# VectorE takes the sums over W2 behind its part of the second block's first einsum

## The chip, the cores and the metric

The kernel runs on one core of one Trainium2 chip. The metric is the time on the device, in microseconds (us), of one execution; the median of several runs is given. TensorE does the matmuls, VectorE (DVE) and ScalarE (ACT) the elementwise work, GpSimd (POOL) casts weights and issues the stores, SyncE (SP) issues the loads.

## The reference, cut to what matters

```
w   = weights[conditions]                     # (128, 64, 64), one matrix for each of 128 samples
xc  = einsum('bct,bcd->bdt', x, w)            # first einsum; x is (128, 64, 512)
W1q = ternarize(W1); W2q = ternarize(W2)      # W1 (2048, 512), W2 (512, 2048)
h   = gelu(einsum('bsd,hd->bsh', xc, W1q) + b1)
y   = einsum('bsd,hd->bsh', h, W2q) + b2
out = x + fp4(y)      # y rounded to multiples of max|y| / 7 + 1e-8

ternarize(W):
    delta = 0.05 * max|W|
    mask  = |W| > delta
    alpha = sum(|W| where mask) / max(count(mask), 1)
    return alpha * sign(W) * mask
```

The kernel keeps the signs (-1, 0 or 1) as weights and applies alpha to the result. So alpha of W2, the sum of the kept magnitudes over their count, is wanted only when the first results y are made.

## The kernel before

*Tiling.* The 128 samples are cut into 16 blocks of 8. A block is four pairs of samples, j = 0 to 3; two samples fill the 128 partitions, and the block has 512 tokens. The hidden layer's 2048 columns are 16 chunks of 128, hc = 0 to 15. W1 and W2 are handled in four groups g of four chunks each.

*Order.* Each engine takes its instructions in the order in which the program writes them. There is no planner: `InOrder` keeps every instruction in program order on its engine, and semaphores join the engines. Moving a line in the program moves that instruction in its engine's queue. As every operation is recorded by that helper, all rows of the profile name line 55; they are told apart by their tiles.

*The first einsum.* `condition(n, j, ...)` is made for each pair: `mix` lets TensorE multiply x by a block-diagonal matrix into a PSUM tile `pc`; ScalarE copies `pc` to the high part `x0`, and VectorE subtracts the high part from `pc` to get the low part `x1` (`split`). In the rows of the profile these are `pc<-diag,xt`, `x<-pc` and `x<-pc,x`. The pool `ps_c` has two PSUM buffers, used by `pc` and by a few small tiles such as `total2`.

*The two layers.* `layer1(n, hc)` multiplies both parts by a chunk of W1 into `ph`; ScalarE applies gelu and VectorE makes the low part of h (`h<-ring,h`); `layer2(n, hc)` multiplies h by a chunk of W2 into four PSUM tiles `py`. POOL widens each chunk of the weights beforehand (`widen1`, `widen2`; rows `wf<-...`), into two or four buffers that TensorE sets free.

*Around the change.* Block 0 is unlike the others: its layer 1 runs while W2 is still being made ternary, so its layer 2 comes afterwards in one loop over hc = 0 to 13 (lines 643 to 666). Beside this loop's matmuls

- VectorE makes the last two groups of W2 ternary (`signed2(2)` at hc = 0, `signed2(3)` at hc = 3; rows `junk<-nat` and `terns<-nat`),
- for each group g, at hc = 4, 6, 8 and 9, ScalarE counts the kept weights (`count2`, rows `masks<-terns`) and stores them in eight bits (`kept`, rows `w2t<-terns`), and VectorE sums them (`sum2`, rows `nat<-nat,terns`, with a read of the accumulator, `sums<-`),
- at hc = 5, 7, 9 and 11 the first einsum of block 1 is done, one pair j each.

Then `eight` goes on with block 1 and the last two chunks of block 0's layer 2. At its second step (`s == NH + 1`) `alpha_2` lets TensorE add the sums and counts over the partitions in a small matmul, `total`; VectorE makes alpha of W2 from it and then the results of block 0.

Of the kernel before, what the change touches and what calls it, by code (L numbers as in the profile page):

```python
# [58 lines left out]
def tile_cond_ternary_ffn(  # L59
# [141 lines left out]
    def parts(n):  # L201
        return [big.tile([P, NT, BLK], F32R, tag="big", name=f"x{k}_{n}") for k in range(2)]

    def split(src, hi, lo, engine=dve):

        act.copy(hi, src)
        engine.tensor_tensor(lo, src, hi, ALU.subtract)

    def pair_of(xt, j):
        return xt[j // 2][:, j % 2, :]  # L210

    def mix(xp, j, pc):

        for c in range(NT):
            pe.matmul(
                out=pc[:, c, :],
                lhsT=xp[:, c * P : (c + 1) * P],
                rhs=diag[:, j, :],
                start=True,
                stop=True,  # L220
            )

    def condition(n, j, xp, two):
        pc = ps_c.tile([P, NT, P], F32, tag="pc", name=f"pc_{n}_{j}")
        mix(xp, j, pc)
        split(pc, *(t[:, :, j * P : (j + 1) * P] for t in two))
# [30 lines left out]
    def flat(w):  # L257
        return w.rearrange("p a b -> p (a b)")
# [130 lines left out]
    def widen2(n, hc):  # L389
        if n == 0 and hc < NH - LAG:  # L390
            w = w2f[hc % 4]
        elif n == NB - 1 and hc == NH - 1:

            w = flat(w1f[0])
        else:
            w = w2f[hc % 2]
        if n == 0 and hc < NH - LAG:
            g, i = divmod(hc, GH)
            pool.tensor_copy(w, group1(terns2, g)[:, i * T : (i + 1) * T])
        else:  # L400
            pool.tensor_copy(w, w2t[:, hc])
        wide2[n, hc] = w
# [28 lines left out]
    def low(n, hc):  # L431

        open_low.pop((n, hc), lambda: None)()

    def layer2(n, hc, js=range(PAIRS)):
        two = hidden[n, hc]
        w = wide2[n, hc]
        if n not in ypsum:
            ypsum[n] = [
                ps_y.tile([P, T], F32, tag=f"py{j}", name=f"py{j}_{n}") for j in range(PAIRS)  # L440
            ]
        for j in js:
            for k in range(2):
                pe.matmul(
                    out=ypsum[n][j],
                    lhsT=two[k][:, j * P : (j + 1) * P],
                    rhs=w,
                    start=(hc == 0 and k == 0),
                    stop=(hc == NH - 1 and k == 1),
                )  # L450
# [56 lines left out]
    def group2(g):  # L507
        return group1(terns2, g)
# [6 lines left out]
    def signed2(g):  # L515

        delta2, minus2 = delta
        below = junk[:, g % 2, :]
        if g % 2 == 0:
            terns2.append(big.tile([P, 2, WCH], BF16, tag="big", name=f"terns2_{g}"))  # L520
        dve.tensor_scalar(below, flat(nat2[g]), minus2, None, ALU.is_lt)
        dve.scalar_tensor_tensor(
            group2(g), flat(nat2[g]), delta2, below, ALU.is_gt, ALU.subtract
        )

    def count2(g):
        act.activation(
            group1(masks, 2 + g % 2), group2(g), AF.Square, accum_out=sums2[:, 1, g : g + 1]
        )

    def sum2(g):
        dve.tensor_tensor_reduce(
            out=flat(nat2[g]),
            in0=flat(nat2[g]),
            in1=group2(g),
            scale=1.0,
            scalar=0.0,
            op0=ALU.mult,
            op1=ALU.add,
            accum_out=sums2[:, 0, g : g + 1],  # L540
        )
# [97 lines left out]
    def kept(t, g, tiles):  # L639

        act.copy(flat(t[:, g * GH : (g + 1) * GH]), group1(tiles, g), saturate=False)

    for hc in range(NH - LAG):
        if hc + 2 < NH - LAG:
            widen2(0, hc + 2)
        layer2(0, hc)
        if hc == 0:
            signed2(2)
        if hc == 1:
            for i in range(10, NH):  # L650
                low(0, i)
        if hc < NG:
            kept(w1t, hc, terns)
        if hc == 3:
            signed2(3)
        if hc == 4:
            two_next = parts(1)
            w2t = big.tile([P, NH, T], F8, tag="big", name="w2t")
        if hc in (4, 6, 8, 9):
            g = {4: 0, 6: 1, 8: 2, 9: 3}[hc]  # L660
            count2(g)
            kept(w2t, g, terns2)
            sum2(g)
        if hc in (5, 7, 9, 11):
            j = (hc - 5) // 2
            condition(1, j, pair_of(x_next, j), two_next)
    cond[1] = two_next
    x_next, two_next, fetched = [], [], []
    hf = ring[:2]
# [296 lines left out]
    while s < len(steps):  # L966
        n, hc = steps[s]
# [133 lines left out]
```

## Time and profile before

| what | value |
|---|---|
| median of 3 runs | 1058.8 us (1058.51 to 1059.65) |
| profiled execution's own time | 1058.49 us |
| its span, first to last instruction | 1056.6 us |
| TensorE busy | 985.9 us, 93% of the span |
| VectorE, ScalarE, POOL busy | 609.9, 612.0 and 625.6 us |
| granted TensorE clock, mean | 0.970; 1.00 in each stretch before 985 us |
| the changed loop's sums on VectorE | four, 2.28 us in the median, from 72.0 to 82.4 us |
| last stage, from about 985 us | loads and stores, TensorE nearly idle |

A row of the profile's order of time gives the start in us, the duration in us, the engine, the line, the operation, what it writes and reads, its shape, and how many alike are merged into it. In square brackets stands how long the engine was idle before it, and what ended that idleness. Rows of one engine overlap a little, since the next instruction begins before the last one's end is recorded. A list of waits gives, for each pair of engine and releaser, the total in us, the number of times and the longest.

### The profile page before, as it was taken

What the parts mean: (1) busy time and instruction counts of PE and PEld (TensorE: products, weight loads), DVE (VectorE), ACT (ScalarE), POOL (GpSimd) and SP (SyncE); (2) the same over time, 40 slices, a digit from 0 to 9 for tenths busy, and PEclk for the clock granted to TensorE, in tenths of its full rate; (3) what the DMA queues carried; (4) which work ended last, traced back from release to release, by engine and by line L of the source; (5) the groups of instructions that cost most, each with busy time, mean ns of one, the idle gap of its engine ahead of it and who ended that gap; (6) DMA issues with size and microseconds to landing.
All of it is one profiled execution on the core that took longest, in us unless ns stands there. A gap on an engine that the chain in (4) does not pass through costs nothing.

```text
span 1056.6 us, 16741 instructions
## 1 busy us (share of the span) xinstructions
PE 985.9 (93%) x5768; PEld 864.5 (82%) x5769; DVE 609.9 (58%) x1081; ACT 612.0 (58%) x1045; POOL 625.6 (59%) x1017
## 2 busy tenths in 40 slices
PE   8999999999999999999999999999999999999500
PEld 5877889999999999999999999999898888888400
DVE  7896645565656565666656565666655223231692
ACT  7993546666666565656666565656555333443591
POOL 6865656676766667676666767576664435333242
PEclk9999999999999999999999999999999999999755
DMA  9100100100000010101000010101001010051799
GB/s 361 59 21 4 32 13 15 31 6 31 15 22 23 14 32 7 39 6 32 15 22 23 14 33 4 41 7 30 16 22 43 3 41 6 1 181 39 264 413 376
DMA packets 26628, 62.21 MB, mean 59 GB/s; under 512 B 3504, under 2 KB 3504, under 8 KB 25776
## 3 DMA queue, kind: packets, MB, share of 16 engines
q1 hardware_dynamic: 19872, 42.25, 12.1%
q0 software_dynamic: 6672, 18.88, 4.7%
q8 instruction: 47, 0.77, 0.3%
q14 instruction: 37, 0.30, 0.1%
HBM read 44.34 MB, written 16.78 MB: 58 GB/s over the span
## 4 chain that ended last, share of the span: by engine, by line
PE 89%; DVE 5%; DMA 3%; ACT 1%; issue 1%; SPq 0%; POOLq 0%; DVEq 0%; ACTq 0%
PE py L55 42%; PE xy L55 16%; PE ph L55 13%; PE z L55 12%; PE pc L55 5%; DMA out<-y 3%; DVE y L55 1%; DVE h L55 1%; ACT diag L55 1%; DMA nat<-in_L_ffn_W 1%; DVE top L55 1%; DVE junk L55 1%; DVE terns L55 0%; PE number L55 0%; DVE ymax L55 0%
## 5 line engine op out<-in xcount | busy, mean ns | idle before, releaser
L55 PE MATMUL py<-wf,h 128*128 128x512 f32 x2048 | 530.7, 395 | 0.0
L55 PEld LDWEIGHTS py<-wf,h 128*128 128x128 f32 x2048 | 365.4, 189 | 63.5 <-DVE y L55 1.9
L55 DVE TENSOR_TENSOR h<-ring,h 128x512 fp32r<-128x512 f32 x236 | 182.7, 777 | 142.7 <-ACT h L55 142.7
L55 POOL CAST wf<-w2t 128x512 fp32r<-128x512 fp8e4 x242 | 169.6, 701 | 152.0 <-PE py L55 148.1
L55 ACT ACTIVATE ring<-ring,b1t,alpha_w 128x512 f32<-128x512 f32 x176 | 144.3, 820 | 97.9 <-DVE ring L55 97.9
L55 POOL CAST wf<-w1s 128x256 fp32r<-128x256 fp8e4 (+1 forms) x264 | 133.8, 511 | 110.2 <-PE xy L55 80.7
L55 POOL CAST wf<-w1t 128x256 fp32r<-128x256 fp8e4 (+1 forms) x240 | 158.5, 665 | 59.4 <-PE ph L55 47.8
L55 PE MATMUL ph<-x,wf 128*128 128x512 f32 (+1 forms) x656 | 157.6, 385 | 0.3 <-DVE x L55 0.3
L55 ACT CAST h<-ring 128x512 fp32r<-128x512 f32 x240 | 148.9, 621 | 7.8
L55 PEld LDWEIGHTS ph<-x,wf 128*128 128x128 f32 x656 | 120.6, 188 | 25.5 <-POOL wf L55 0.7
L55 DVE TENSOR_TENSOR ring<-xy,ring 128x256 f32<-128x256 f32 (+1 forms) x176 | 97.3, 553 | 64.3 <-PE xy L55 64.3
L55 PEld LDWEIGHTS xy<-xt,wf 128*128 128x128 f32 x704 | 107.6, 189 | 14.1
L55 PE MATMUL xy<-xb,wf 128*128 128x256 f32 x704 | 112.4, 281 | 0.0
L55 PE MATMUL xy<-xt,wf 128*128 128x256 f32 x704 | 111.8, 282 | 0.0
L55 ACT ACTIVATE ring<-ph,b1t,alpha_w 128x512 f32<-128x512 f32 x64 | 49.8, 778 | 106.3 <-PE ph L55 106.2
L55 PEld LDWEIGHTS xy<-xb,wf 128*128 128x128 f32 x704 | 102.2, 190 | 7.9
L55 ACT COPY ring<-xy 128x256 f32<-128x256 f32 x176 | 65.1, 370 | 68.1 <-PE xy L55 68.0
L55 PE MATMUL z<-xt,wf 128*128 128x256 f32 x704 | 98.3, 282 | 0.0
L55 ACT COPY ring<-z 128x512 f32<-128x512 f32 x88 | 51.7, 588 | 73.6 <-DVE h L55 71.4
L55 PEld LDWEIGHTS z<-xt,wf 128*128 128x128 f32 x704 | 90.2, 190 | 0.0
L55 DVE TENSOR_TENSOR xt<-x_quarters,xt 128x512 fp32r<-128x512 f32 x44 | 33.8, 767 | 90.9 <-ACT xt L55 90.9
L55 POOL DMA_INDIRECT wg<-in_L_cond_weights,rows x64 | 73.2, 1143 | 11.8 <-issue 7.7
(108 smaller groups left out, 886.8 us busy)
## 6 DMA issues: line engine op xcount, KB each, us to landing
xt<-in_x SPq DMA_DIRECT2D x36, 512.0 KB, 7.0
out<-y POOLq DMA_DIRECT2D x29, 512.0 KB, 12.3
x_quarters<-in_x SPq DMA_DIRECT2D x48, 256.0 KB, 2.6
nat<-in_L_ffn_W SPq DMA_DIRECT2D x6, 1024.0 KB, 10.3
nat<-in_L_ffn_W SPq DMA_DIRECT2D x3, 512.0 KB, 8.8
wg<-in_L_cond_weights,rows POOLq DMA_INDIRECT x64, 2.7
w1t<-in_x SPq DMA_DIRECT2D x4, 256.0 KB, 2.7
w2t<-in_x SPq DMA_DIRECT2D x4, 256.0 KB, 2.6
```

Of the source, the lines that this page charges most:

```text
L55: return lambda *args, **kw: self._tc.keep_in_program_order(make(*args, **kw))
```

## The change

The call of `sum2(g)` at hc = 4, 6, 8 and 9 is taken out. The sums are now called behind `condition(1, j)`: the sum of group 0 behind j = 1 (hc = 7), of group 1 behind j = 2 (hc = 9), of groups 2 and 3 behind j = 3 (hc = 11). `count2` and `kept` stay where they were. As `count2`, `kept` and `condition` keep their order, only VectorE's queue changes.

```diff
@@ -660,10 +660,11 @@
             g = {4: 0, 6: 1, 8: 2, 9: 3}[hc]
             count2(g)
             kept(w2t, g, terns2)
-            sum2(g)
         if hc in (5, 7, 9, 11):
             j = (hc - 5) // 2
             condition(1, j, pair_of(x_next, j), two_next)
+            for g in {7: [0], 9: [1], 11: [2, 3]}.get(hc, []):
+                sum2(g)
     cond[1] = two_next
     x_next, two_next, fetched = [], [], []
     hf = ring[:2]
```

VectorE's order in this part, from the end of `signed2(3)` on:

| before | after |
|---|---|
| sum2(0), low part j = 0 | low part j = 0, low part j = 1 |
| sum2(1), low part j = 1 | sum2(0), low part j = 2 |
| sum2(2), sum2(3) | sum2(1), low part j = 3 |
| low part j = 2, low part j = 3 | sum2(2), sum2(3) |

## The prediction

> **What bounds the kernel now.** I read three views in this order: busy time and the chain of waits, for what sets the end; what TensorE waited for, for its holes; and the order of time around the largest hole, engine by engine.
>
> ```profile
> PE 985.9 (93%) x5768; PEld 864.5 (82%) x5769; DVE 609.9 (58%) x1081; ACT 612.0 (58%) x1045; POOL 625.6 (59%) x1017
> PE 89%; DVE 5%; DMA 3%; ACT 1%; issue 1%; SPq 0%; POOLq 0%; DVEq 0%; ACTq 0%
> ...
> PE pc L55 <- DVE x L55: 1.2, 1, 1.2
> ```
>
> TensorE carries 89% of the chain and is busy nearly without a break up to the tail that starts near 985 us, so only its own work and holes count. The list of its waits has one hole inside the dense part that this edit can touch: a first-einsum matmul (`pc`) of block 1 that waited 1.2 us, once, for a VectorE subtract into `x`. Its place on TensorE:
>
> ```profile
> 65.25 3.89 PE L55 MATMUL py<-wf,h 128*128 128x512 f32 x16
> 68.98 1.05 PE L55 MATMUL pc<-diag,xt 128*128 128x128 f32 x8
> 69.79 3.89 PE L55 MATMUL py<-wf,h 128*128 128x512 f32 x16
> 74.90 1.16 PE L55 MATMUL pc<-diag,xt 128*128 128x128 f32 x8 [1.23 <-DVE x L55]
> 75.81 3.89 PE L55 MATMUL py<-wf,h 128*128 128x512 f32 x16
> 79.54 1.05 PE L55 MATMUL pc<-diag,xt 128*128 128x128 f32 x8
> 80.35 3.89 PE L55 MATMUL py<-wf,h 128*128 128x512 f32 x16
> ```
>
> These are `layer2(0, hc)` two at a time, with `mix` for j = 1, 2, 3 between. And VectorE's queue:
>
> ```profile
> 69.39 2.64 DVE L55 SCALAR_TENSOR_TENSOR terns<-nat,delta_w,junk 128x2048 bf16<-128x2048 f32 x1
> 71.95 2.28 DVE L55 CUSTOM_DVE_ANT_0 nat<-nat,terns 128x2048 f32<-128x2048 f32 x1
> ...
> 74.17 0.68 DVE L55 TENSOR_TENSOR x<-pc,x 128x512 fp32r<-128x512 f32 x1
> 74.77 2.63 DVE L55 CUSTOM_DVE_ANT_0 nat<-nat,terns 128x2048 f32<-128x2048 f32 x1
> ...
> 82.36 1.27 DVE L55 TENSOR_TENSOR x<-pc,x 128x512 fp32r<-128x512 f32 x2
> ```
>
> `CUSTOM_DVE_ANT_0` is `sum2`; `x<-pc,x` is the low part of `condition`, call them lo0 to lo3. `ps_c` has two buffers, so the third `pc` can't start until lo0 has read the first. lo0 ends at 74.85 and the `pc` starts at 74.90. lo0 was late because `sum2(0)` stood in front of it. ScalarE's copy that lo0 also needs was done at 66.58 (66.00 + 0.58), so nothing else held it.
>
> **The change part by part.** It adds and removes nothing: four `sum2`, their four accumulator reads and four lo subtracts only trade places on VectorE. The queues of TensorE, ScalarE, POOL and SP keep their order, so no DMA is moved. The new VectorE order is lo0, lo1, sum2(0), lo2, sum2(1), lo3, sum2(2), sum2(3).
>
> *What goes.* lo0 runs at 71.95 (0.68) and lo1 at 72.55, both buffers are free by 73.22, and TensorE comes to the third `pc` at 69.79 + (68.98 - 65.25) = 73.52. It no longer waits. From one `py` row to the next took 80.35 - 75.81 = 4.54 undisturbed and 75.81 - 69.79 = 6.02 with the hole: gain 1.48 us (the 1.23 of the wait, and what weight loads and the pipeline lost around it). From there on every TensorE row shifts by 1.48, if nothing new holds it.
>
> *What comes late instead.* lo2 now stands in front of three sums, and lo2 waits for ScalarE, whose queue is full and keeps its times:
>
> ```profile
> 76.25 1.90 ACT L55 CAST w2t<-terns 128x2048 fp8e4<-128x2048 bf16 x1
> 78.05 0.59 ACT L55 CAST x<-pc 128x512 fp32r<-128x512 f32 x1
> 80.63 0.59 ACT L55 CAST x<-pc 128x512 fp32r<-128x512 f32 x1 [2.00 <-PE pc L55]
> ```
>
> So VectorE idles from about 75.5 to 78.66, then lo2 (next start 0.60 later), sum2(1) at 79.26, lo3 at 81.47 (a sum with its read costs 2.21 from start to start, 80.15 to 82.36), done at 82.15; sum2(2) at 82.07, sum2(3) at 84.28, its read done at 86.56. The third ScalarE copy shown moves up with TensorE to 79.15 and is done before lo3. Two places on TensorE need these:
>
> - `layer1(1, 0)`, the first `ph`, at 84.07 - 1.48 = 82.59; its second matmul (82.82) reads lo3's part. lo3 is 0.67 us early.
> - the matmul `total` of `alpha_2`, at 89.51 - 1.48 = 88.03, needs sum2(3). It is 1.47 us early if no sum is slowed.
>
> *Sums beside POOL's casts.* In the trace a sum and a cast don't overlap:
>
> ```profile
> 75.21 2.67 POOL L55 CAST wf<-w1t 128x512 fp32r<-128x512 fp8e4 x1
> ```
>
> This cast of 0.61 us lasted until 77.88, just past the end of the sum of 74.77 to 77.40; and that sum took 2.63 where two others took 2.27 and 2.28, so it lost 0.35 to a cast before it. The Trainium skill, "SBUF — State Buffer", "Who interferes with whom", says more, and it speaks against the change: whichever of two such instructions starts first keeps the shared port for its whole length, so a sum behind a cast can lose all of its 0.61. The sums now lie where casts are released (81.10, 82.89 and 84.70 in shifted time), sum2(2) and sum2(3) above all. By the row each loses 0.35 and the last read ends at 87.26; by the rule each loses 0.61, and it ends at 87.78; both are before 88.03, so the sum of the prediction is the same 1.48. Only if two casts pass in a row in front of one of them does it end near 88.4, and 0.4 us of the gain goes. I take the row, and keep 0.4 for the range. The subtracts aren't slowed: the two at 82.36 took 1.27 together beside two casts of 0.62 (at 82.58 and 83.14).
>
> The other direction, casts behind sums: `widen2(0, 14)` would end near 82.0 and is needed at 84.41; `widen1(1, 1)` near 82.6, needed 86.22; `widen2(0, 15)` near 85.2, needed 88.17; `widen1(1, 2)` near 87.9, needed 90.10; `widen2(1, 0)` near 88.5, needed 92.04. All are covered by two us or more. Without that cover a blocked cast would cost up to 2.1 us (2.67 - 0.61).
>
> *Queued behind the sums on VectorE.* The subtract of h for (1, 0), at 86.13 in shifted time, starts about 1.2 later. `layer2(1, 0)` reads it at 92.04, and the next subtract isn't due before 89.70: nothing. The results of block 0 and the small stalls on `py` at 91 to 96 follow that later subtract and TensorE, and only shift.
>
> *The sum.* -1.48 us and nothing given back. Against the profiled execution's own time: 1058.49 - 1.48 = 1057.01. That execution is 0.3 below the median of the runs, 1058.8, so the median comes to 1057.3, or -0.14%. The tail is started by TensorE's last `py`, and its loads and stores by its buffers; I let it shift whole.
>
> **The rivals.**
>
> *The gain is partly given back at `total`.* Place: sum2(3), 0.8 us (row) or 0.25 us (rule) ahead of TensorE. For it: three of four sums now run after 79 us, and casts are dense there. Each cast more that passes in front of a sum costs up to 0.61, so the time is 1057.5 to 1058.8.
>
> *Slower: lo2 holds the sums too long.* All three later sums are queued behind lo2, and lo2 behind ScalarE's `w2t` cast. If ScalarE's copy of the third `pc` came d later than 78.05, sum2(3) comes d later, and TensorE stands still at `total` for d - 0.8. It decides from d = 2.3 (no gain left); at d = 4.5 it is 2.2 us slower, 1061.0. For it: this wait is new, and one subtract carries three sums. Against: ScalarE ran from 55.10 to 78.6 without a hole, on data that VectorE delivers as before (`terns` of the last group ends at 72.03, the count that reads it starts at 74.35, 2.3 us later), and neither sums nor subtracts touch what it waits for.
>
> *It doesn't do what it says.* The third `pc` also waits for the load of its half of x. If that were the true releaser, nothing would change: 1058.8. The load was issued at about 42 and loads of this kind landed in 7.0 us, so it had long been there.
>
> *Faster than reckoned.* A measured median moves too: the three runs span 1.14 us. With 0.6 us of that on the gain's side, 1056.6.
>
> **How the numbers follow.** What a measurement of this kernel can tell from no change is about 0.2%, 2.1 us; the forecast of 1.5 us lies inside. Forecast as summed: 0.68. Part given back: 0.11. No effect: 0.04. Over 2.1 us faster, by the spread of runs or a tail that falls better: 0.12. Slower than before by over 0.2%: 0.05. The first three are the 0.83 of "same", of which I move 0.04 to "faster" and 0.02 to "slower", since the forecast lies only 0.6 us from the bound on the one side and a tail of 70 us of transfers may fall either way: 0.16, 0.77, 0.07. The range takes in 0.4 us given back, the spread of the runs on either side, and the case of no effect: 1056.1 to 1059.0.
>
> **What would show it.** In the profile of the changed kernel: no wait of `pc` for `x` in TensorE's list; the third `pc` at about 73.5, the first `ph` of block 1 at 82.6, `total` near 88.0, and the last `py` 1.5 us earlier. VectorE idle for some 3 us ahead of lo2, released by ScalarE; the last sum's read ending at 86.6 to 87.8. Wrong if TensorE waits for `sums` ahead of `total`, or for `x` ahead of the first `ph`; or if the shift is there at 90 us and gone at 985.

## The result, and the profile after

| | before | after |
|---|---|---|
| median | 1059.08 us (15 runs, 1058.51 to 1060.14) | 1057.24 us (15 runs, 1056.78 to 1057.75) |
| ratio | 1 | 0.9983, 95% interval 0.9976 to 0.9989 |
| span of the profiled execution | 1056.6 us | 1055.8 us |

The kernel is 1.84 us faster, with an interval of 1.2 to 2.5 us (the ratio's ends times 1059). That is clear of no change. The 1.84 lies inside the 0.2%, or 2.1 us, that the prediction called "same"; the upper end of the interval doesn't.

First TensorE's list of waits after the change (releaser; total us, times, longest). The wait of `pc` for `x` is gone, and no line has come in its place. (The 0.3 us of `ph` for `x` belong to block 0, at 21 us, and were there before.)

```profile
PE idle L55 <- POOL junk L55: 3.0, 1, 3.0
PE tops_scale L55 <- DVE diag L55: 2.2, 1, 2.2
PE ph L55 <- DVE x L55: 0.3, 1, 0.3
```

Then the order of time on TensorE, from the second `pc` of block 1 to the results of block 0. The columns are start, duration, engine, line, operation:

```profile
69.07 1.05 PE L55 MATMUL pc<-diag,xt 128*128 128x128 f32 x8
69.87 3.89 PE L55 MATMUL py<-wf,h 128*128 128x512 f32 x16
73.60 1.05 PE L55 MATMUL pc<-diag,xt 128*128 128x128 f32 x8
...
82.66 1.98 PE L55 MATMUL ph<-x,wf 128*128 128x512 f32 x8
...
88.10 0.28 PE L55 MATMUL total<-sums,ones_f 128*128 128x8 f32 x2
88.24 2.09 PE L55 MATMUL py<-wf,h 128*128 128x512 f32 x8
90.17 1.99 PE L55 MATMUL ph<-x,wf 128*128 128x512 f32 x8
92.10 2.62 PE L55 MATMUL py<-wf,h 128*128 128x512 f32 x8
94.56 2.00 PE L55 MATMUL ph<-x,wf 128*128 128x512 f32 x8
...
983.43 5.63 PE L55 MATMUL py<-wf,h 128*128 128x512 f32 x24
```

Three of these rows in the kernel before:

```profile
84.07 1.98 PE L55 MATMUL ph<-x,wf 128*128 128x512 f32 x8
...
89.51 0.28 PE L55 MATMUL total<-sums,ones_f 128*128 128x8 f32 x2
...
984.95 5.63 PE L55 MATMUL py<-wf,h 128*128 128x512 f32 x24
```

From the second `pc` to the first `ph` of block 1 it is 13.59 us (82.66 - 69.07), where it was 15.09 (84.07 - 68.98): 1.50 gained in this stretch. The gain is still there at the last 24 `py`, which start 1.52 earlier. The two profiled spans differ by only 0.8 us, because the stretch from there to the end took 72.4 us in this execution and 71.7 in the one before. Over the traces of all the kernels here that stretch varies from 71.6 to 72.4 us, so a single span can't weigh a gain of this size.

And VectorE's queue:

```profile
72.04 1.27 DVE L55 TENSOR_TENSOR x<-pc,x 128x512 fp32r<-128x512 f32 x2
73.24 2.27 DVE L55 CUSTOM_DVE_ANT_0 nat<-nat,terns 128x2048 f32<-128x2048 f32 x1
...
78.75 0.69 DVE L55 TENSOR_TENSOR x<-pc,x 128x512 fp32r<-128x512 f32 x1 [3.23 <-ACT x L55]
79.36 2.28 DVE L55 CUSTOM_DVE_ANT_0 nat<-nat,terns 128x2048 f32<-128x2048 f32 x1
...
81.56 0.68 DVE L55 TENSOR_TENSOR x<-pc,x 128x512 fp32r<-128x512 f32 x1
82.17 2.65 DVE L55 CUSTOM_DVE_ANT_0 nat<-nat,terns 128x2048 f32<-128x2048 f32 x1
...
84.74 2.69 DVE L55 CUSTOM_DVE_ANT_0 nat<-nat,terns 128x2048 f32<-128x2048 f32 x1
87.36 0.08 DVE L55 DVE_READ_ACCUMULATOR2_ANT sums<- 128x1 f32 x1
```

The new idle time of 3.23 us ahead of lo2 costs nothing (e5_filled, below, shows it); the last sum's read ends at 87.44, 0.66 us before TensorE comes to `total`.

### The profile page after: what moved, and what is told of

Read it like the earlier page. It is cut to its first block, busy times and chain, and to the rows that moved or that the text cites. A ratio compares the mean times of both kernels' runs of the same rounds, so it can differ in the third digit from the quotient of the medians.

```text
span 1055.8 us, 16743 instructions
## 1 busy us (share of the span) xinstructions
PE 986.1 (93%) x5769; PEld 864.8 (82%) x5769; DVE 610.2 (58%) x1081; ACT 611.6 (58%) x1045; POOL 625.6 (59%) x1017
## 4 chain that ended last, share of the span: by engine, by line
PE 93%; DMA 3%; DVE 1%; ACT 1%; issue 0%; POOL 0%; POOLq 0%; DVEq 0%; ACTq 0%
PE py L55 44%; PE xy L55 16%; PE ph L55 14%; PE z L55 12%; PE pc L55 5%; DMA xt<-in_x 2%; PE idle L55 1%; DMA out<-y 1%; ACT diag L55 1%; DVE y L55 1%; PE number L55 0%; DVE ymax L55 0%; DVE py L55 0%; POOLq L1098 0%; DVE x L55 0%
## 5 line engine op out<-in xcount | busy, mean ns | idle before, releaser
L55 POOL CAST wf<-w2t 128x512 fp32r<-128x512 fp8e4 x242 | 172.3, 712 | 152.7 <-PE py L55 148.8
L55 POOL CAST wf<-w1s 128x256 fp32r<-128x256 fp8e4 (+1 forms) x264 | 131.1, 501 | 111.5 <-PE xy L55 80.9
```

The source lines that it names most:

```text
L55: return lambda *args, **kw: self._tc.keep_in_program_order(make(*args, **kw))
```

## The experiments

Ratios are to the kernel before on the same chip, with 95% intervals. "lo" is the low part that VectorE makes for one pair of block 1.

**One sum alone (e1_one_sum).** Only the sum of group 0 goes behind lo0.

```diff
             kept(w2t, g, terns2)
-            sum2(g)
+            if g > 0:
+                sum2(g)
...
             condition(1, j, pair_of(x_next, j), two_next)
+            if j == 0:
+                sum2(0)
```

> Only the sum of group 0 is moved, behind the low part of j = 0; the other three sums stay where they were. VectorE's order: low 0, sums 0 and 1, low 1, sums 2 and 3, low 2, low 3. Theory A (the hole at the third pc is all that counts, whatever follows): the whole gain, 1.5 us. Theory B (the subtracts are deadlines: the gain moves TensorE 1.4 us forward to the first ph of block 1, and that one needs the low part of j = 3, which now ends as late as before, near 83.6): the third pc no longer waits, but TensorE waits about 0.7 us at the first ph, and the gain is only 0.6 to 0.9 us. Rival C (the sums moved back are what helps, by taking the port from POOL at another time): no gain, since three of four stay.

Measured: 1058.43 us, ratio 0.9994 (0.9987 to 1.0), 0.6 us by the medians. TensorE, order of time:

```profile
73.50 1.05 PE L55 MATMUL pc<-diag,xt 128*128 128x128 f32 x8
...
78.22 1.16 PE L55 MATMUL pc<-diag,xt 128*128 128x128 f32 x8
...
82.88 0.39 PE L55 MATMUL ph<-x,wf 128*128 128x512 f32 x1
83.84 1.88 PE L55 MATMUL ph<-x,wf 128*128 128x512 f32 x7 [0.57 <-DVE x L55]
...
89.18 0.28 PE L55 MATMUL total<-sums,ones_f 128*128 128x8 f32 x2
```

The hole at the third `pc` has gone (73.50), and most of the gain is taken back where the first `ph` stops after one matmul, the one that reads only high parts, until lo3 is there at 83.78. A small wait of the fourth `pc` for lo1 takes some too: that row starts at 78.22, 4.72 after the third `pc`, where it is 4.53 in the changed kernel. From the second `pc` (68.96) to `total` it takes 20.22 us, 0.31 less than before (89.51 - 68.98 = 20.53); the changed kernel gains 1.50 there. So theory B has the mechanism right, but less is left than its 0.6 to 0.9: 1.19 of the 1.50 are lost, more than the waits in the rows (0.19 and 0.57) add up to. Theory A falls: more than the first sum had to move. Rival C, that the port to POOL matters, is better judged by the next run, in which no sum moves.

**Another buffer (e2_other_buffer).** VectorE's order as before; the third `pc` gets a PSUM buffer that isn't in use.

```diff
     def condition(n, j, xp, two):
-        pc = ps_c.tile([P, NT, P], F32, tag="pc", name=f"pc_{n}_{j}")
+        if (n, j) == (1, 2):
+            pc = ps_h.tile([P, NT, P], F32, tag="ph", name=f"pc_{n}_{j}")
+        else:
+            pc = ps_c.tile([P, NT, P], F32, tag="pc", name=f"pc_{n}_{j}")
```

> VectorE's order is that of the kernel before; only the third pc of block 1 is put into a PSUM buffer of ps_h, so that it waits for no subtract. If the wait for a free buffer was the cause of the hole, the third pc starts at 73.6 as in the changed kernel. Theory B: then the first ph of block 1 comes to 82.7 and waits for the low part of j = 3 (83.6), so the gain is 0.6 to 0.9 us, as in the run with one sum moved. Theory A: 1.5 us. If the load of x or anything else was the true releaser of the third pc: 0.0.

Measured: 1058.58 us, ratio 0.9995 (0.9986 to 1.0003); on the clock alone not told from no change, so the trace decides. TensorE:

```profile
73.39 1.05 PE L55 MATMUL pc<-diag,xt 128*128 128x128 f32 x8
...
83.58 1.90 PE L55 MATMUL ph<-x,wf 128*128 128x512 f32 x7 [0.73 <-DVE x L55]
...
88.96 0.28 PE L55 MATMUL total<-sums,ones_f 128*128 128x8 f32 x2
```

The third `pc` starts 4.53 after the second (68.86), with no wait, although nothing on VectorE has moved. So the buffer that lo0 had to empty was the cause of the hole, not the load of x, and not where the sums stand beside POOL's casts (rival C). And the same second wait appears, 0.73 us for lo3: from the second `pc` to `total` 0.43 us are gained (88.96 - 68.86 = 20.10), again less than forecast.

**All sums last (e3_sums_last).** The four sums stand behind lo3.

```diff
             kept(w2t, g, terns2)
-            sum2(g)
...
             condition(1, j, pair_of(x_next, j), two_next)
+            if j == 3:
+                for g in range(NG):
+                    sum2(g)
```

> All four sums behind the low part of j = 3: the subtracts are as early as they can be, the sums as late. The hole at the third pc is gone and the first ph waits for nothing. The sums start near 80.5 and four of them at 2.21 to 2.65 end at 89.3 to 91.0, where TensorE comes to total at 88.1: it waits there 1.2 to 2.9 us. If total is the deadline of the sums, as the prediction has it, the time is 0.3 us below to 1.5 us above that of the kernel before. If the sums have room beyond total (alpha is wanted only by the results at 91), the gain stays 1.5 us.

Measured: 1060.05 us, ratio 1.0012 (1.0004 to 1.002): 1.0 us slower than before, within what was forecast if `total` is the deadline. TensorE:

```profile
86.72 1.98 PE L55 MATMUL ph<-x,wf 128*128 128x512 f32 x8
91.16 0.36 PE L55 MATMUL total<-sums,ones_f 128*128 128x8 f32 x2 [2.47 <-DVE sums L55]
```

`total` waits 2.47 us for the last sum, so it is the sums' deadline. Three of the four sums took 2.69 us here, beside three casts of 2.67 each.

**The changed kernel again, sums fitted in, and alpha earlier.** Four runs share this question: is anything left? In e5_filled the order is lo0, sum 0, lo1, sums 1 and 2, lo2, lo3, sum 3, so that VectorE sums while it would wait for ScalarE. e4_alpha_early, and once more e7_alpha_again, add this to it:

```diff
-        if s == NH + 1:
+        if s == NH:
             alpha_2()
```

Against the changed kernel the sums of e5_filled are called so:

```diff
             j = (hc - 5) // 2
+            if hc == 9:
+                sum2(2)
             condition(1, j, pair_of(x_next, j), two_next)
-            for g in {7: [0], 9: [1], 11: [2, 3]}.get(hc, []):
+            for g in {5: [0], 7: [1], 11: [3]}.get(hc, []):
                 sum2(g)
```

> The sums are fitted into VectorE's idle time (low 0, sum 0, low 1, sums 1 and 2, low 2, low 3, sum 3, the last ending near 84), and alpha_2 is called one step earlier, so that total stands at 84.5 and alpha is there before the subtract of h for chunk 1 of block 1. The results of block 0 then start near 90.4 where they started at 91.2 in the changed kernel, and the stalls of py behind them (0.64 and 0.12 us, seen as a py group of 2.62 us where 1.98 is usual) go. If those stalls come from the wait of that subtract ahead of alpha: 0.5 to 0.8 us faster than the changed kernel, 2.0 to 2.3 faster than the kernel before. If they come from the pace of the four results (0.66 us each against 0.45 of TensorE): as the changed kernel. If the last sum isn't done at 84.5: slower than the changed kernel by what it is late.

> The changed kernel once more, on the same chip as the three beside it. Ratio to the kernel before 0.9980 to 0.9988; TensorE's row of py behind the results of block 0 keeps its 2.62 us.

> The sums fitted into VectorE's idle time (low 0, sum 0, low 1, sums 1 and 2, low 2, low 3, sum 3), alpha_2 where it was. The last sum ends near 84 where it ended at 87.4 in the changed kernel. If VectorE's idle 3.2 us and the thin margin at total cost nothing, as the prediction says: the same time as the changed kernel within 0.3 us. If sums beside POOL's casts cost TensorE something that the waits don't show: 0.3 to 0.8 us faster.

> The kernel with fitted sums and alpha_2 one step earlier, on the same chip as the changed kernel. Its trace showed the py group behind the results at 2.15 us in place of 2.62 and the gap from total's py to the next ones closed: 0.6 us in all. If that comes through to the end: 0.4 to 0.8 us faster than the changed kernel, ratio to before 0.9973 to 0.9980. If it is lost later: as the changed kernel.

| kernel | median | ratio | 95% interval |
|---|---|---|---|
| after_again | 1057.44 | 0.9984 | 0.9978 to 0.9991 |
| e5_filled | 1057.16 | 0.9983 | 0.9976 to 0.9989 |
| e4_alpha_early (run with the first three) | 1056.89 | 0.9976 | 0.9966 to 0.9986 |
| e7_alpha_again | 1056.76 | 0.9979 | 0.9971 to 0.9986 |

e5_filled is the changed kernel within 0.3 us: neither VectorE's idle 3.2 us nor the sums beside the casts cost anything that the median can tell. It also shows that not all sums had to stand late: there only the last one comes behind lo3. With alpha earlier the results of block 0 hold up `py` less. TensorE in e7_alpha_again:

```profile
69.35 1.05 PE L55 MATMUL pc<-diag,xt 128*128 128x128 f32 x8
...
84.76 0.28 PE L55 MATMUL total<-sums,ones_f 128*128 128x8 f32 x2
...
90.46 1.98 PE L55 MATMUL ph<-x,wf 128*128 128x512 f32 x8
92.28 2.15 PE L55 MATMUL py<-wf,h 128*128 128x512 f32 x8
94.27 1.98 PE L55 MATMUL ph<-x,wf 128*128 128x512 f32 x8
```

Of the waits of `py`'s weight loads for these results (0.30, 0.36 and 0.36 us in the changed kernel) one of 0.31 is left. The `py` of 2.62 us is 2.15 now, and from `pc` 2 to this last `ph` it takes 24.92 us (94.27 - 69.35) against 25.49 in the changed kernel (94.56 - 69.07): 0.57 gained. The median is 0.68 below that of after_again. The intervals overlap, so the time by itself shows this version faster than before by 2.3 us, and only the trace shows it faster than the changed kernel.

**The changed order with alpha earlier (e6_after_alpha).** The same edit of `alpha_2`, on the changed kernel.

> The changed kernel's order of sums, with alpha_2 one step earlier, so that total stands at 84.5 where the last sum is done at 87.4. If total is the sums' deadline: TensorE waits there 2.9 us (less a few tenths, since POOL's casts no longer come between), gains the 0.6 us of the earlier results, and the kernel is 0.5 to 1.0 us slower than before (1.9 to 2.5 slower than the changed kernel). If the sums had more room than reckoned: as fast as the kernel with fitted sums.

Measured: 1061.23 us, ratio 1.0019 (1.0013 to 1.0026), 2.2 us slower than before. The direction and the wait are as expected, the size isn't (0.5 to 1.0 slower than before). TensorE, order of time:

```profile
87.42 0.38 PE L55 MATMUL total<-sums,ones_f 128*128 128x8 f32 x2 [2.94 <-DVE sums L55]
87.65 3.65 PE L55 MATMUL py<-wf,h 128*128 128x512 f32 x8
91.13 2.00 PE L55 MATMUL ph<-x,wf 128*128 128x512 f32 x8
```

The busy times by stretch of the same kernel (from:to, its length, busy time of PE, PEld, DVE, ACT and POOL; then the granted clock, third from the end):

```profile
84.00:87.40 3.40, 0.48 (x3) 0.07 (x2) 3.40 (x5) 1.40 (x2) 3.40 (x2) 1.00 0.00 0
87.40:89.00 1.60, 1.58 (x5) 1.39 (x6) 1.43 (x5) 0.00 (x0) 0.33 (x1) 0.57 0.00 0
89.00:90.00 1.00, 1.00 (x4) 0.73 (x3) 0.00 (x0) 0.00 (x0) 0.00 (x0) 0.50 0.00 0
90.00:91.00 1.00, 1.00 (x4) 0.81 (x3) 0.00 (x0) 0.00 (x0) 0.00 (x0) 0.50 0.00 0
91.00:92.00 1.00, 1.00 (x5) 0.83 (x5) 0.00 (x0) 0.00 (x0) 0.57 (x1) 0.98 0.00 0
```

Eight `py` matmuls took 3.65 us in place of 2.09, 1.56 more: behind the wait TensorE ran at half its clock for about 3.5 us. The five runs of this kernel with the highest mean clock (0.970) took 1059.3 to 1059.9 us, 0.3 to 0.8 above the kernel before, near what was expected; the other sixteen took 1060.87 or more.

**TensorE kept busy (e8_kept_busy).** Twelve matmuls that nobody reads are put into that wait.

```diff
         if s == NH:
+            busy = ps_c.tile([P, T], F32, tag="pc", name="busy")
+            for _ in range(12):
+                pe.matmul(out=busy, lhsT=ones_b, rhs=group2(0)[:, :T], start=True, stop=True)
             alpha_2()
```

> As the changed order with alpha_2 one step earlier (e6_after_alpha), and 12 matmuls more that nobody reads, of ones against 512 columns of the ternary W2, ahead of total, where TensorE stood still for 2.9 us. They take about 0.22 us each, 2.6 us in all, and end before the last sum. In e6_after_alpha the eight py matmuls behind that wait took 3.65 us where 2.09 is usual, at a granted clock of 0.50, and 16 of its 21 runs lay at 1060.9 us or above, 5 at 1059.3 to 1059.9. If the lower clock comes from the idleness: the clock stays at 1.00 behind total, py takes 2.1 us, and the median is near 1059.7, 1.5 below e6_after_alpha, without the upper group. If it comes from something else in that place (the port, the small matmul): as e6_after_alpha, 1061.2.

Measured: 1059.85 us, ratio 1.001 (1.0002 to 1.0018). It ran on another chip than e6_after_alpha; against the kernel before on its own chip it is 1.0 us slower, where e6_after_alpha was 2.2, although it does more work. The two intervals overlap, so the trace and the clock of the runs have to decide. TensorE, order of time:

```profile
84.53 2.76 PE L55 MATMUL busy<-terns,ones_b 128*128 128x512 bf16 x12
87.64 0.36 PE L55 MATMUL total<-sums,ones_f 128*128 128x8 f32 x2 [0.34 <-DVE sums L55]
87.85 2.09 PE L55 MATMUL py<-wf,h 128*128 128x512 f32 x8
```

And its stretches behind the wait, as above:

```profile
87.40:89.00 1.60, 1.36 (x7) 1.22 (x8) 1.50 (x6) 0.00 (x0) 0.56 (x1) 1.00 0.00 0
89.00:91.00 2.00, 2.00 (x11) 1.65 (x10) 0.16 (x1) 0.00 (x0) 0.62 (x1) 1.00 0.00 0
```

The clock stays at 1.00, `py` is back at 2.09, and twelve of the 13 runs have a mean clock of 0.970 or more, where five of 21 had it in e6_after_alpha. The port and the small matmul were there as before, so the lower clock came from the idleness. (Three of the 13 runs still took 1060.5 to 1060.9 us, two of them at 0.970; what made them slower isn't known.)

## Why the prediction was right

- *The hole and its cause.* As forecast: third `pc` at 73.60 (forecast about 73.5), first `ph` at 82.66 (82.6), `total` at 88.10 (88.0). e2_other_buffer shows that the buffer was the cause, and so refutes the rival that a load released the `pc`.
- *Its size.* 1.48 by the rows, 1.50 found there. From the second `pc` to the start of the last 24 `py` it is 1.61 (984.95 - 68.98 against 983.43 - 69.07); where the other 0.1 came from stays open. The medians fell by 1.84 and, on another occasion, by 1.63; both intervals hold 1.5. That the median came within 0.1 us of the forecast 1057.3 is in part luck: the kernel before turned out to take 1059.08, not 1058.8, and the fall was larger than reckoned by about as much. The row of the pattern (from one `py` to the next, with and without the hole) was the better measure than the wait's own 1.23.
- *The two deadlines.* lo3 was forecast 0.67 us early, at 82.15; it ended at 82.24 (81.56 + 0.68), early enough. e1_one_sum and e2_other_buffer show that this deadline was real: with lo3 where it was before, only 0.3 to 0.4 of the 1.50 us are left at `total`. The prediction had named the place, but not that moving the first sum alone would fail by it.
- *Sums beside casts.* By the row each of two late sums was to lose 0.35, by the rule on the shared port up to 0.61. They took 2.65 and 2.69, 0.4 above 2.28: nearer to the row. The prediction's words that a sum and a cast don't overlap are loose: their rows do overlap. What both traces show is that a cast begun while a sum ran ends about 0.5 us after it: `widen1(1, 2)` was forecast to end near 87.9 and ended at 87.91 (85.24 + 2.67), the sum beside it at 87.43.
- *The rivals.* Nothing was given back at `total`. The slower rival, sums too late at `total`, didn't come about, but e3_sums_last and e6_after_alpha show its place to be right. Its price was too simple: the prediction took each microsecond of lateness for one of time, and a wait of 2.9 us cost some 1.5 us more through the clock. The rival "faster than reckoned", more than 2.1 us by the spread of the runs, didn't come about either.

## What to carry to other kernels

When one engine's queue feeds another from two kinds of work, ask of each piece when it is needed, and put the one with the near deadline first: here a subtract held a PSUM buffer that TensorE wanted at once, and the sums were wanted 15 us later. Removing one wait moves everything behind it up, and so makes the next deadline nearer by as much; look for the instruction that is late then, before moving only the one in front (e1_one_sum kept 0.3 us of 1.5 by its trace, 0.6 by the medians). Price a hole by the pattern with and without it, not by the wait alone.

## What the runs showed of the hardware

I had not expected that a single wait of 2.9 us inside a busy stretch would halve TensorE's clock. In the profiled execution of e6_after_alpha it did: granted clock 0.50 to 0.57 from 87.4 to 91.0 us, and 1.56 us lost on `py`. It doesn't seem to happen every time: of 21 runs five kept a mean clock of 0.970, and sixteen had 0.967 to 0.969. (3.5 us at half clock are 0.0017 of the span, which is about that difference.) For a single run the mean is a weak sign, since the changed kernel run again, without such a wait, shows 0.969 in three of 21. With 2.5 us of waiting, e3_sums_last kept its clock at 1.00 in the profile, and five of its 13 runs show 0.968 or 0.969 and 1060.6 us or more; whether the wait did that isn't shown. The Trainium skill, "TensorE: Matmul & The Clock Gate", "What's actually happening", gives the halved clock after at least one idle window of about 3.4 us, and says that the window runs freely. Here a wait of 2.94 us was enough. That it came in some runs and not in others would fit a freely running window, but no run here tests that.
